# A quantised feed-forward stage written as turns, with five sequences under way and its wide rounding on another engine

## The chip, the core and the metric

The kernel runs on one core of a Trainium2 chip. The core has five engines, each with its own queue of instructions that it works through in order: TensorE (PE) multiplies matrices, VectorE (DVE), ScalarE (ACT) and GpSimd (POOL) work element by element, SyncE (SP) issues transfers between the main memory and SBUF, the on-chip memory. PE writes into PSUM, eight banks of 128 x 512 floats. Engines wait for one another by semaphores. The metric is the device time of one execution in microseconds (us).

## The reference, cut to what is touched

The model is a small decoder of two layers over 16 sequences of 128 positions and 1024 features. Its six parts run one after the other; each adds its result to its input and normalises. The third part, the feed-forward of the first layer, is the one that the change touches:

```python
def _dynamic_quant(x, inv_smooth):
    xs = x.astype(jnp.float32) * inv_smooth
    scale = jnp.maximum(jnp.max(jnp.abs(xs), axis=-1, keepdims=True) / QMAX, 1e-08)
    q = jnp.clip(jnp.round(xs / scale), -QMAX, QMAX)
    return (q, scale)
...
x_flat = x.reshape(-1, H).astype(jnp.bfloat16)
qg, sg = _dynamic_quant(x_flat, inv_gate)
qu, su = _dynamic_quant(x_flat, inv_up)
gate_out = _quant_gemm(qg, sg, w_gate, s_wgate)
up_out = _quant_gemm(qu, su, w_up, s_wup)
inter = jax.nn.silu(gate_out) * up_out
inter = jnp.clip(inter, -SWIGLU_LIMIT, SWIGLU_LIMIT).astype(jnp.bfloat16)
qi, si = _dynamic_quant(inter, inv_inter)
out = _quant_gemm(qi, si, w_down, s_wdown)
...
x = _layernorm(x + _L0_ffn_ref(x, ...), axis=-1)
```

H is 1024, the inner width 512, QMAX 127. So each position's row is turned into integers between -127 and 127 with a scale of its own, three times: for the gate product, for the up product, and for the down product.

## The kernel before

The stage `stage_quant` works on one sequence at a time: a tile of 128 positions (partitions) by 1024 features. It has no integer arithmetic; integers are floats that hold whole numbers, and each weight matrix is held as two parts (`w[n][0]`, `w[n][1]`) whose products are summed. For one sequence b it does this:

- `integers(b)`: SP loads x (line 60, four buffers); ACT casts it to bf16, xb (L669); for gate and for up POOL multiplies it by inv_gate or inv_up into xs (L673), and `quantise` follows on DVE: the maximum of the absolute values of a row, am (L603), the scale sc (L605), its reciprocal rc (L607), and the rounding (L608), which multiplies by rc and adds 12582912, so that the addition itself rounds.
- `first`: for gate and for up, `transposed` turns the 1024 columns in eight pieces of 128 (PE, L619) into two PSUM tiles t of four pieces each. ACT subtracts the constant again and writes the first half of qt (L621), DVE the second half (L623). Sixteen matmuls (L685: eight pieces of the contraction, two weight parts) give acc, 128x512. DVE scales gate's acc to g (L688), ACT applies silu (L689), DVE scales up's acc to u (L691), POOL multiplies g by u (L692), DVE clips to bf16, ib (L694), POOL multiplies by inv_inter to it (L696), and `quantise` runs over it.
- `second`: it is turned (four pieces, ACT writes qi, L621), sixteen matmuls over two halves of 512 columns give o (L705), DVE scales it to r (L708), POOL adds x (L709), and `layer_norm` finishes: DVE takes statistics in two halves (L85), their aggregate (L87) and the variance plus epsilon (L89), POOL takes the root ln_rs (L91), DVE normalises into x (L92). SP stores x (L711).

The loop takes a sequence's integers one step ahead, runs `first` of sequence b, then `second` of b-1. This is the order in which the program is written; a scheduler then orders each engine's instructions by its own estimate, except where the program ties them. `Ctx.ordered` (line 43) does that tying elsewhere in the kernel: it notes where it was called, and when the function that it returns is called, it ties every instruction of the given engines, written in between, to the one written before it on the same engine. `stage_quant` doesn't use it.

Pools hold the tiles in a number of buffers (`bufs`): a tile may be written once the tile that many places before it has been read to the end. Of PSUM, t has three banks, acc three, o two.

The stage before it (attention to a context, `stage_cross`) writes x1 to main memory, from where `stage_quant` loads; the stage after it (`stage_gqa`) loads x2, which `stage_quant` stores, and the memory of the weights of `stage_quant` is given free for its weights.

Of the kernel before, what the change touches and what calls it, by code (L numbers as in the profile page):

```python
# [23 lines left out]
P = 128  # L24
NB = 16
NT = NB * P
HID = 1024
# [4 lines left out]
class Ctx:  # L32
# [24 lines left out]
    def load(self, pool, src, b, tag="x", bufs=3):  # L57

        x = self.t(pool, [P, HID], tag, bufs=bufs)
        self.nc.sync.dma_start(x, src[b])  # L60
        return x
# [15 lines left out]
    return v.rearrange("(o n) -> o n", o=1).to_broadcast([parts, v.shape[0]])  # L77


def layer_norm(K, pool, src, dst):  # L80

    nc = K.nc
    st = K.t(pool, [P, 2, 6], "ln_st", bufs=2)
    for i in range(2):
        nc.vector.bn_stats(st[:, i, :], src[:, i * 512:(i + 1) * 512])  # L85
    mv = K.t(pool, [P, 2], "ln_mv", bufs=2)
    nc.vector.bn_aggr(mv, st.rearrange("p a b -> p (a b)"))  # L87
    ve = K.t(pool, [P, 1], "ln_ve", bufs=2)
    nc.vector.tensor_scalar(ve, mv[:, 1:2], LN_EPS, None, ALU.add)  # L89
    rs = K.t(pool, [P, 1], "ln_rs", bufs=2)  # L90
    nc.gpsimd.tensor_tensor(rs, ve, K.neghalf, ALU.pow)  # L91
    nc.vector.tensor_scalar(dst, src, mv[:, 0:1], rs, ALU.subtract, ALU.mult)  # L92

# [403 lines left out]
def stage_cross(K, rise, xmid, dst, piece):  # L497
# [6 lines left out]
    with ExitStack() as st:  # L504
# [3 lines left out]
        def risen(b):  # L508

            x, r = rise.got[b]  # L510
            if b + 2 < NB:
                rise.fetch(b + 2)
            for i in range(2):
                cols = slice(i * 512, (i + 1) * 512)
                pu = K.t(ps, [P, 512], "pu")
                nc.tensor.matmul(pu, xmid[:, b * P:(b + 1) * P], w["up"][:, cols], start=True, stop=True)
                nc.vector.tensor_tensor(r[:, cols], pu, r[:, cols], ALU.add)
            layer_norm(K, work, r, x)
            return x
# [54 lines left out]
        for b in range(NB):  # L574
            r = K.t(work, [P, HID], "ro")
            for i in range(2):
                if i == 0 and b + 1 < NB:
                    x1, kv1 = risen(b + 1), context(b + 1)
                nxt = None
                if i == 0:  # L580
                    nxt = attention(x, kv, 1)
                elif b + 1 < NB:
                    nxt = attention(x1, kv1, 0)
                attended(x, kv, i, ex, r)
                ex = nxt
            layer_norm(K, work, r, x)
            nc.scalar.dma_start(dst[b], x)
            piece(b)
            x, kv = (x1, kv1) if b + 1 < NB else (None, None)
# [3 lines left out]
MAGIC = 12582912.0  # L593
FFI = 512


def quantise(K, work, xs):

    nc = K.nc
    am = K.t(work, [P, 1], "am", bufs=4)
    nc.vector.tensor_reduce(am, xs, AX.X, ALU.max, apply_absolute_value=True)  # L603
    sc = K.t(work, [P, 1], "sc", bufs=6)
    nc.vector.tensor_scalar(sc, am, 1.0 / 127.0, 1e-8, ALU.mult, ALU.max)  # L605
    rc = K.t(work, [P, 1], "rc", bufs=4)
    nc.vector.reciprocal(rc, sc)  # L607
    nc.vector.tensor_scalar(xs, xs, rc, MAGIC, ALU.mult, ALU.add)  # L608
    return sc


def transposed(K, work, ps, q, n, tag, bufs=2):

    nc = K.nc
    qt = K.t(work, [P, n // P, P], tag, F32R, bufs=bufs)
    for h in range(n // 512):
        pt = K.t(ps, [P, 4, P], "t", bufs=3)
        for k in range(4):
            nc.tensor.transpose(pt[:, k, :], q[:, (4 * h + k) * P:(4 * h + k + 1) * P], K.ident)  # L619
        if h == 0:  # L620
            nc.scalar.activation(qt[:, 4 * h:4 * h + 4, :], pt, AF.Identity, bias=K.negmagic)  # L621
        else:
            nc.vector.tensor_scalar(qt[:, 4 * h:4 * h + 4, :], pt, MAGIC, None, ALU.subtract)  # L623
    return qt


def parts(K, hi, lo, v, eng):
# [30 lines left out]


def stage_quant(K, w, v, src, dst):  # L660
    nc, a = K.nc, K.a
    with ExitStack() as st:
        work = K.pool(st, "f_work", 2)
        ps = K.pool(st, "f_ps", 1, PSUM)
        def integers(b):

            x = K.load(work, src, b, bufs=4)
            xb = K.t(work, [P, HID], "xb", BF16)
            nc.scalar.copy(xb, x)  # L669
            qs = []  # L670
            for n in ("gate", "up"):
                xs = K.t(work, [P, HID], "xs", bufs=4)
                nc.gpsimd.tensor_tensor(xs, xb, v["inv_" + n], ALU.mult)  # L673
                qs.append((xs, quantise(K, work, xs)))
            return x, qs

        def first(x, qs):

            acc = []
            for (xs, _), n in zip(qs, ("gate", "up")):  # L680
                qt = transposed(K, work, ps, xs, HID, "qt")
                pa = K.t(ps, [P, FFI], "acc", bufs=3)
                for k in range(8):
                    for i in range(2):
                        nc.tensor.matmul(pa, qt[:, k, :], w[n][i][:, k, :], start=(k + i == 0), stop=(k + i == 8))  # L685
                acc.append(pa)
            g = K.t(work, [P, FFI], "g")
            nc.vector.scalar_tensor_tensor(g, acc[0], qs[0][1], v["s_wgate"], ALU.mult, ALU.mult)  # L688
            nc.scalar.activation(g, g, AF.Silu)  # L689
            u = K.t(work, [P, FFI], "u")  # L690
            nc.vector.scalar_tensor_tensor(u, acc[1], qs[1][1], v["s_wup"], ALU.mult, ALU.mult)  # L691
            nc.gpsimd.tensor_tensor(g, g, u, ALU.mult)  # L692
            ib = K.t(work, [P, FFI], "ib", BF16)
            nc.vector.tensor_scalar(ib, g, 10.0, -10.0, ALU.min, ALU.max)  # L694
            it = K.t(work, [P, FFI], "it")
            nc.gpsimd.tensor_tensor(it, ib, v["inv_inter"], ALU.mult)  # L696
            return x, it, quantise(K, work, it)

        def second(b, x, it, si):
            qt = transposed(K, work, ps, it, FFI, "qi", bufs=1)  # L700
            po = K.t(ps, [P, 2, 512], "o")
            for h in range(2):
                for k in range(4):
                    for i in range(2):
                        nc.tensor.matmul(po[:, h, :], qt[:, k, :], w["down"][i][:, k, h * 512:(h + 1) * 512],  # L705
                                         start=(k + i == 0), stop=(k + i == 4))
            r = K.t(work, [P, HID], "r", bufs=1)
            nc.vector.scalar_tensor_tensor(r, po.rearrange("p a b -> p (a b)"), si, v["s_wdown"], ALU.mult, ALU.mult)  # L708
            nc.gpsimd.tensor_tensor(r, r, x, ALU.add)  # L709
            layer_norm(K, work, r, x)  # L710
            nc.sync.dma_start(dst[b], x)  # L711


        ahead = integers(0)
        waiting = None
        for b in range(NB):
            now = ahead
            if b + 1 < NB:
                ahead = integers(b + 1)
            now = first(*now)  # L720
            if b:
                second(b - 1, *waiting)
            waiting = now
        second(NB - 1, *waiting)

# [538 lines left out]
class Front:  # L1264
# [62 lines left out]
    def product(self, l, bank):  # L1327
        t, j = self.place(l)
        if t < 0:
            return False  # L1330
        self.part(t, j, bank)
        if l == FIRST_ROUTED:
            self.first = routed(self.K, self.W, self.keep, lambda shape, tag: bank(shape, "gq"), self.xT[2], 1)
        return True
# [26 lines left out]
    def scaled(self, t, h):  # L1361

        nc, (raw, dst) = self.nc, self.scales[t]
        sl = slice(h * 512, (h + 1) * 512)
        hi = self.W["hi"]
        nc.vector.tensor_copy(hi, raw[:, sl])
        nc.vector.scalar_tensor_tensor(dst[:, sl], hi.bitcast(F32), self.lohi, raw[:, sl], ALU.mult, ALU.add)
# [499 lines left out]
```

## Time and profile before

| | us |
|---|---|
| median of three executions | 3445.27 (3441.66 to 3451.8) |
| the profiled execution, its own time | 3442.97 |
| its span | 3441.2 |
| busy in the span: PE, DVE, ACT, POOL | 3100.6, 1852.5, 1410.7, 898.8 |
| the stage: first cast of x to the end of the last normalisation | 596.36 to 905.77 |
| busy from 619.67 to 875.37: PE, DVE, ACT, POOL | 214.2, 173.4, 49.1, 131.2 |

The span is the time from the first to the last instruction in the profile. In the page's rows of slices the span is cut into 40 equal parts of 86 us; a digit is the busy share of an engine in tenths, and PEclk is the clock that PE was granted, in tenths of the full one. A row of windows gives a stretch, its length, and busy time and number of instructions of PE, its weight loads (PEld), DVE, ACT and POOL, then the granted clock, the busy share of the DMA engines and GB/s. A row of a group gives line, engine, operation, the tile written and the tiles read, shapes and count; then busy us and the mean of one in ns; then the engine's idle time just before these instructions and what ended it. A row of waits reads: who waited for whom, us in total, times, the longest. A row of the timeline: start and duration in us, engine, line, operation, tiles, count, and in brackets the idle time before it and what ended it.

Mean durations of single instructions in the stage (us): maximum of 128x1024 1.22, of 128x512 0.69; rounding of xs 0.85, of it 1.08 (0.48 at the least, 2.07 at the most); POOL's spreading of xs 2.15 to 2.24, its addition of x 2.40, g*u 1.29, it 1.17, root 0.55; ACT's cast 1.04, halves of qt 0.69, silu 0.63.

### The profile page before, as it was taken

The page shows a single profiled execution, that of the slowest core. Times are in us where ns is not written, and L with a number is a line of the kernel's source. Part 1 is how long each engine was busy: PE and PEld are TensorE (multiplying, and loading weights), DVE is VectorE, ACT ScalarE, POOL GpSimd, SP SyncE. Part 2 cuts the span into 40 slices and gives each one's busy share as a digit, 9 for nine tenths or more (in the row PEclk, how much of TensorE's full clock was granted, in tenths as well). Part 3 has the DMA queues.
Part 4 walks back from the last instruction along what each step waited for, and adds up shares of the span by engine and source line. Part 5 has one row for each costly group of instructions (what it writes and reads, how often), then busy time and mean ns, then how long its engine had stood idle before and what let it go on. Part 6 is the DMA issues. An engine that isn't in the chain of part 4 may idle for free.

```text
span 3441.2 us, 62967 instructions
## 1 busy us (share of the span) xinstructions
PE 3100.6 (90%) x24917; PEld 1679.0 (49%) x24917; DVE 1852.5 (54%) x5211; ACT 1410.7 (41%) x3610; POOL 898.8 (26%) x1087
## 2 busy tenths in 40 slices
PE   7887786888799999999998999999999999999998
PEld 3444453666455555555454444444444444444465
DVE  5875775666334454545233455555555555555555
ACT  3443432221132232334122555555555555555533
POOL 3334764455333233233011011111111111111122
PEclk8887998899899999998999999999999999999999
DMA  5001322111400010103221100000000000000044
GB/s 193 1 1 36 114 77 104 37 49 62 168 25 25 19 43 25 50 13 98 89 66 59 42 23 30 29 23 29 23 29 23 23 17 23 17 17 14 25 131 104
DMA packets 97216, 170.23 MB, mean 49 GB/s; under 512 B 14362, under 2 KB 55194, under 8 KB 96922
## 3 DMA queue, kind: packets, MB, share of 16 engines
q1 hardware_dynamic: 92858, 157.10, 14.4%
q10 hardware_dynamic: 4064, 9.11, 0.7%
q8 instruction: 197, 3.23, 0.4%
q14 instruction: 97, 0.79, 0.1%
HBM read 115.83 MB, written 51.64 MB: 49 GB/s over the span
## 4 chain that ended last, share of the span: by engine, by line
PE 57%; ACT 9%; DVE 6%; issue 2%; DMA 0%; POOL 0%; SPq 0%; DVEq 0%; POOLq 0%; ACTq 0%
PE p L794 8%; ACT th L1085 8%; PE s L1176 7%; PE pf L1070 7%; PE p L865 6%; PE p L1013 3%; PE m L1625 3%; PE gq L1212 3%; PE ff L1191 2%; PE t L843 2%; PE s L822 2%; PE p L807 2%; PE ff L1089 2%; PE s L1120 2%; PE c L854 1%
## 5 line engine op out<-in xcount | busy, mean ns | idle before, releaser
L1085 ACT ACTIVATE th<-pf 128x512 f32<-128x512 f32 x512 | 264.4, 602 | 276.9 <-PE pf L1070 276.8
L831 ACT ACTIVATE s<-s,nm 128x128 f32<-128x128 f32 x512 | 198.3, 389 | 251.7 <-DVE nm L828 221.7
L1205 POOL COPY hist<-gT 128x16 f32<-128x16 f32 x256 | 42.6, 198 | 934.9 <-DVE gT L1203 934.9
L1176 PE MATMUL s<-hb,aD 128*32 128x256 f32 x4096 | 276.1, 387 | 0.6 <-DVE aD L1164 0.6
L865 PE MATMUL p<-ga_Wo,cT 128*128 128x512 f32 x512 | 228.7, 595 | 0.0
L1158 ACT COPY pf<-enc 128x512 f32<-128x512 f32 x381 | 224.6, 590 | 8.1
L794 PE MATMUL p<-xT,ga_Wq 128*128 128x512 f32 x512 | 226.4, 597 | 0.0
L834 POOL TENSOR_TENSOR s<-s,rs 128x512 f32<-128x512 f32 x128 | 133.3, 1041 | 320.9 <-DVE rs L833 315.2
L1070 PE MATMUL pf<-R,waf 32*128 32x160 f32 x2032 | 181.4, 426 | 33.9 <-DVE R L1228 33.7
L794 PEld LDWEIGHTS p<-xT,ga_Wq 128*128 128x128 f32 x512 | 95.4, 190 | 113.8 <-issue 111.0
L865 PEld LDWEIGHTS p<-ga_Wo,cT 128*128 128x128 f32 x512 | 93.8, 190 | 113.8 <-issue 111.7
L1176 PEld LDWEIGHTS s<-hb,aD 128*32 128x32 f32 x4096 | 106.7, 109 | 84.3 <-DVE aD L1164 45.8
L1094 DVE TENSOR_REDUCE nm<-s 128x1 f32<-128x128 f32 x128 | 37.4, 292 | 203.3 <-PE s L1089 203.3
L1196 ACT ACTIVATE fs<-ff,rx 128x384 f32<-128x384 f32 x127 | 73.8, 581 | 173.2 <-DVE rx L1194 171.6
L1089 PE MATMUL s<-th,vaE 128*32 128x128 f32 x2048 | 109.0, 286 | 36.0 <-ACT th L1085 27.8
L845 DVE COPY pT<-t 128x512 f32<-128x512 f32 x128 | 87.9, 687 | 91.0 <-PE t L843 90.8
L1070 PEld LDWEIGHTS pf<-R,waf 32*128 32x128 f32 x2032 | 79.3, 182 | 99.4 <-DVE R L1228 74.2
L1089 PE MATMUL ff<-th,vaE 128*32 128x128 f32 x2048 | 109.6, 287 | 16.2
L91 POOL TENSOR_TENSOR ln_rs<-ln_ve,neghalf 128x1 f32<-128x1 f32 x64 | 37.9, 597 | 309.0 <-DVE ln_ve L89 292.3
L1013 PE MATMUL p<-xT,qT 128*128 128x512 f32 x256 | 115.8, 606 | 0.3 <-ACT qT L1008 0.2
L866 DVE TENSOR_TENSOR xr<-p,xr 128x512 f32<-128x512 f32 x32 | 22.1, 692 | 168.9 <-PE p L865 168.9
L685 PE MATMUL acc<-w_up,qt 128*128 128x512 f32 x256 | 79.6, 462 | 36.7 <-DVE qt L623 33.4
(392 smaller groups left out, 6794.8 us busy)
## 6 DMA issues: line engine op xcount, KB each, us to landing
x<-x SPq DMA_DIRECT2D x79, 512.0 KB, 3.6
xt<-xT SPq DMA_DIRECT2D x8, 1024.0 KB, 7.6
x<-x ACTq DMA_DIRECT2D x16, 512.0 KB, 2.6
xr<-x SPq DMA_DIRECT2D x16, 512.0 KB, 3.7
x<-xr SPq DMA_DIRECT2D x16, 512.0 KB, 2.6
x<-x SPq DMA_DIRECT2D x128, 64.0 KB, 2.4
xb<-r SPq DMA_DIRECT2D x16, 512.0 KB, 3.0
xb<-xb SPq DMA_DIRECT2D x16, 512.0 KB, 4.0
```

The costliest lines, as they stand in the source:

```text
L794: nc.tensor.matmul(pq, lhsT, xT[:, k].rearrange("p i t -> p (i t)"), start=(k == 0), stop=(k == 7))
L831: nc.scalar.activation(s[:, r, :], s[:, r, :], AF.Exp, bias=nm[:, r:r + 1], accum_out=sm[:, r:r + 1])
L834: nc.gpsimd.tensor_tensor(s, s, rs.unsqueeze(2).to_broadcast([P, 4, P]), ALU.mult)
L865: nc.tensor.matmul(po, cT[:, k, :], w["o"][h][:, k, :], start=(k == 0), stop=(k == 7))
L1013: nc.tensor.matmul(py, xT[:, k, b % 4, :], ys[:, k, :], start=(k == 0), stop=(k == 7))
L1070: nc.tensor.matmul(pf[:, k, first:first + n].rearrange("p b t -> p (b t)"), lhs[32 * k:32 * k + 32, :], rhs[32 * k:32 * k + 32, 32 * first ...
L1085: nc.scalar.activation(th.rearrange("p i (k t) -> p i k t", t=32), pf[:, :, 4 * g:4 * g + 4, :].rearrange("p k i t -> p i k t"), AF.Tanh)
L1089: nc.tensor.matmul(pe[32 * i:32 * i + 32, :], D["va"][:, 31 - b:63 - b], th[:, i, :], start=False, stop=(g % 2 == 1), skip_group_check=True)
L1158: nc.scalar.copy(pf[:, k], D["enc"][:, k])
L1176: nc.tensor.matmul(pg[32 * i:32 * i + 32, :], aD[:, 4 * g + i, :], D["hb"][:, 4 * g + i, :], start=(g == 0), stop=(g == 3), skip_group_che ...
L1212: nc.tensor.matmul(gq[32 * q:32 * q + 32, :], gT[:, c].rearrange("p e b -> p (e b)"), D["gs"][:, c, q * P:(q + 1) * P], start=False, stop= ...
L1625: nc.tensor.matmul(pm[:, h, :], xp[:, k, :], w[:, k, h * 512:(h + 1) * 512], start=(k + n == 0), stop=(k + n == 8))
```

## The change

The loop over sequences is replaced by turns. Turn b (from -2 to 17) handles parts of five sequences: the root, normalisation and store of b-2, the integers and the down product of b-1, both products of b, the integers of b+1, the cast and gate's spreading of b+2, and the load of b+3. PE, DVE, ACT and POOL are tied to the order in which the turn is written. Within a turn, the integers of the up product of b are turned before its gate product, those of the middle (it, of b-1) between the gate and the up product, and those of gate of b+1 before the down product of b-1. The rounding of xs goes from DVE to ACT (an Identity activation with rc as scale and the constant as bias, both columns of 128x1); the rounding of it stays on DVE. `quantise` and `transposed` become `scales` (without the rounding) and `turn` (which hands back the second half's subtraction, to be written later). `layer_norm` is split into `norm_sums` and `norm_root`, with unchanged instructions. x has five buffers instead of four, sc eight instead of six, and a column holding the constant is added.

```diff
+def norm_sums(K, pool, src):
...
+    return mv, ve
+def norm_root(K, pool, ve):
     rs = K.t(pool, [P, 1], "ln_rs", bufs=2)
+    K.nc.gpsimd.tensor_tensor(rs, ve, K.neghalf, ALU.pow)
+    return rs
...
-def quantise(K, work, xs):
+def scales(K, work, xs):
...
-    sc = K.t(work, [P, 1], "sc", bufs=6)
+    sc = K.t(work, [P, 1], "sc", bufs=8)
...
-    nc.vector.tensor_scalar(xs, xs, rc, MAGIC, ALU.mult, ALU.add)
-    return sc
+    return sc, rc
...
+        own = K.pool(st, "f_own", 1)
+        magic = K.t(own, [P, 1], "magic")
+        nc.vector.memset(magic, MAGIC)
+        X, XB, XS, SC, QT, ACC, G, U, IT, QI, O, R, MV, RS = ({} for _ in range(14))
+        def load(b):
+            X[b] = K.load(work, src, b, bufs=5)
+        def cast(b):
+            XB[b] = K.t(work, [P, HID], "xb", BF16)
+            nc.scalar.copy(XB[b], X[b])
+        def spread_out(b, n):
+            XS[b, n] = K.t(work, [P, HID], "xs", bufs=4)
+            nc.gpsimd.tensor_tensor(XS[b, n], XB[b], v["inv_" + n], ALU.mult)
+        def scaled(b, n):
+            SC[b, n], rc = scales(K, work, XS[b, n])
+            nc.scalar.activation(XS[b, n], XS[b, n], AF.Identity, bias=magic, scale=rc)
+        def turn(q, n, tag):
+            qt = K.t(work, [P, n // P, P], tag, F32R, bufs=2 if n > 512 else 1)
+            pts = []
+            for h in range(n // 512):
+                pt = K.t(ps, [P, 4, P], "t", bufs=3)
+                for k in range(4):
+                    nc.tensor.transpose(pt[:, k, :], q[:, (4 * h + k) * P:(4 * h + k + 1) * P], K.ident)
+                pts.append(pt)
+            nc.scalar.activation(qt[:, 0:4, :], pts[0], AF.Identity, bias=K.negmagic)
+            return qt, lambda: nc.vector.tensor_scalar(qt[:, 4:8, :], pts[1], MAGIC, None, ALU.subtract)
...
+        order = K.ordered((mybir.EngineType.PE, mybir.EngineType.DVE, mybir.EngineType.Activation, mybir.EngineType.Pool))
+        for b in range(3):
+            load(b)
+        for b in range(-2, NB + 2):
+            now, back, done, soon, far = (0 <= c < NB for c in (b, b - 1, b - 2, b + 1, b + 2))
+            if done:
+                R[b - 2] = K.t(work, [P, HID], "r", bufs=1)
+                nc.vector.scalar_tensor_tensor(R[b - 2], O[b - 2].rearrange("p a b -> p (a b)"), SC[b - 2, "it"], v["s_wdown"],
+                                               ALU.mult, ALU.mult)
+            if now:
+                QT[b, "up"], rest = turn(XS[b, "up"], HID, "qt")
+            if back:
+                SC[b - 1, "it"], rc = scales(K, work, IT[b - 1])
+                nc.vector.tensor_scalar(IT[b - 1], IT[b - 1], rc, MAGIC, ALU.mult, ALU.add)
+            if now:
+                rest()
+            if done:
+                nc.gpsimd.tensor_tensor(R[b - 2], R[b - 2], X[b - 2], ALU.add)
+            if soon:
+                scaled(b + 1, "gate")
+            if now:
+                product(b, "gate")
+            if soon:
+                spread_out(b + 1, "up")
+            if now:
+                G[b] = K.t(work, [P, FFI], "g")
+                nc.vector.scalar_tensor_tensor(G[b], ACC[b, "gate"], SC[b, "gate"], v["s_wgate"], ALU.mult, ALU.mult)
+            if back:
+                QI[b - 1], _ = turn(IT[b - 1], FFI, "qi")
+            if now:
+                nc.scalar.activation(G[b], G[b], AF.Silu)
+            if far:
+                cast(b + 2)
+            if soon:
+                scaled(b + 1, "up")
+            if now:
+                product(b, "up")
+            if done:
+                mv, ve = norm_sums(K, work, R[b - 2])
+                rs = norm_root(K, work, ve)
+            if far:
+                spread_out(b + 2, "gate")
+            if now:
+                U[b] = K.t(work, [P, FFI], "u")
+                nc.vector.scalar_tensor_tensor(U[b], ACC[b, "up"], SC[b, "up"], v["s_wup"], ALU.mult, ALU.mult)
+            if soon:
+                QT[b + 1, "gate"], rest = turn(XS[b + 1, "gate"], HID, "qt")
+            if now:
+                nc.gpsimd.tensor_tensor(G[b], G[b], U[b], ALU.mult)
+            if back:
+                product_down(b - 1)
+            if soon:
+                rest()
+            if done:
+                nc.vector.tensor_scalar(X[b - 2], R[b - 2], mv[:, 0:1], rs, ALU.subtract, ALU.mult)
+                nc.sync.dma_start(dst[b - 2], X[b - 2])
+            if 3 <= b + 3 < NB:
+                load(b + 3)
+            if now:
+                ib = K.t(work, [P, FFI], "ib", BF16)
+                nc.vector.tensor_scalar(ib, G[b], 10.0, -10.0, ALU.min, ALU.max)
+                IT[b] = K.t(work, [P, FFI], "it")
+                nc.gpsimd.tensor_tensor(IT[b], ib, v["inv_inter"], ALU.mult)
+        order()
```

`product` and `product_down` hold the matmuls of `first` and `second` as they were.

More of the change, by code (lines that the diff above doesn't have):

```diff
@@ L77, in spread @@
     return v.rearrange("(o n) -> o n", o=1).to_broadcast([parts, v.shape[0]])
-def layer_norm(K, pool, src, dst):
+def norm_sums(K, pool, src):
     nc = K.nc
@@ L89, in layer_norm @@
     nc.vector.tensor_scalar(ve, mv[:, 1:2], LN_EPS, None, ALU.add)
+    return mv, ve
+def norm_root(K, pool, ve):
     rs = K.t(pool, [P, 1], "ln_rs", bufs=2)
-    nc.gpsimd.tensor_tensor(rs, ve, K.neghalf, ALU.pow)
-    nc.vector.tensor_scalar(dst, src, mv[:, 0:1], rs, ALU.subtract, ALU.mult)
+    K.nc.gpsimd.tensor_tensor(rs, ve, K.neghalf, ALU.pow)
+    return rs
+def layer_norm(K, pool, src, dst):
+    mv, ve = norm_sums(K, pool, src)
+    K.nc.vector.tensor_scalar(dst, src, mv[:, 0:1], norm_root(K, pool, ve), ALU.subtract, ALU.mult)
 HY_L = 16
@@ L607, in quantise @@
     nc.vector.reciprocal(rc, sc)
-    nc.vector.tensor_scalar(xs, xs, rc, MAGIC, ALU.mult, ALU.add)
-    return sc
[L612 to L624, printed above, removed]
+    return sc, rc
 def parts(K, hi, lo, v, eng):
@@ L660, in stage_quant @@
 def stage_quant(K, w, v, src, dst):
-    nc, a = K.nc, K.a
+    nc = K.nc
     with ExitStack() as st:
@@ L664, in stage_quant @@
         ps = K.pool(st, "f_ps", 1, PSUM)
[L665 to L697, printed above, removed]
@@ L699, in second @@
-        def second(b, x, it, si):
-            qt = transposed(K, work, ps, it, FFI, "qi", bufs=1)
-            po = K.t(ps, [P, 2, 512], "o")
+        own = K.pool(st, "f_own", 1)
[7 more added lines that the diff above has]
+            nc.scalar.copy(XB[b], X[b])
@@ L702, in second, with product, product_down @@
+        def product(b, n):
+            ACC[b, n] = K.t(ps, [P, FFI], "acc", bufs=3)
+            for k in range(8):
+                for i in range(2):
+                    nc.tensor.matmul(ACC[b, n], QT[b, n][:, k, :], w[n][i][:, k, :], start=(k + i == 0), stop=(k + i == 8))
+        def product_down(b):
+            O[b] = K.t(ps, [P, 2, 512], "o")
             for h in range(2):
@@ L704, in second @@
                     for i in range(2):
-                        nc.tensor.matmul(po[:, h, :], qt[:, k, :], w["down"][i][:, k, h * 512:(h + 1) * 512],
+                        nc.tensor.matmul(O[b][:, h, :], QI[b][:, k, :], w["down"][i][:, k, h * 512:(h + 1) * 512],
                                          start=(k + i == 0), stop=(k + i == 4))
-            r = K.t(work, [P, HID], "r", bufs=1)
-            nc.vector.scalar_tensor_tensor(r, po.rearrange("p a b -> p (a b)"), si, v["s_wdown"], ALU.mult, ALU.mult)
@@ L709, in second @@
[L709 to L724, printed above, removed]
+        order = K.ordered((mybir.EngineType.PE, mybir.EngineType.DVE, mybir.EngineType.Activation, mybir.EngineType.Pool))
```

## The prediction, made before the changed kernel ran

> **What bounds the kernel now.** The page first, for where the stage lies: by the windows it runs from about 596 us (first input there) to 905.8 us, slices 7 to 10, and there neither PE nor its clock is full.
>
> ```profile
> PE   7887786888799999999998999999999999999998
> PEclk8887998899899999998999999999999999999999
> ```
>
> Next the windows. The repeating part goes from the gate product of sequence 1 (its first matmul starts at 619.68) to that of sequence 15 (875.38): 14 turns in 255.7 us, 18.26 us each.
>
> ```profile
> core 0: us, PE busy (x) PEld busy (x) DVE busy (x) ACT busy (x) POOL busy (x), PEclk, DMA share, GB/s
> ...
> 619.67:875.37 255.70, 214.22 (x949) 166.65 (x949) 173.38 (x318) 49.13 (x68) 131.17 (x82) 0.93 0.15 52
> ...
> 863.46:866.87 3.41, 1.17 (x6) 0.61 (x4) 2.64 (x7) 0.00 (x0) 2.02 (x2) 1.00 0.00 0
> 866.87:870.28 3.41, 3.23 (x8) 2.56 (x9) 2.96 (x7) 0.63 (x1) 0.00 (x1) 0.50 0.38 154
> ```
>
> Per turn: PE 15.3 busy of 18.3, DVE 12.4, POOL 9.4, ACT 3.5. PE is the fullest and still idles 3 us a turn, and the last two rows show what follows: in a 3.41 us window PE works 1.17 us, and in the next its clock is 0.50. So an idle stretch costs twice. The groups and waits of the stage (600 to 905 us) say who makes it idle:
>
> ```profile
> L685 PE MATMUL acc<-w_up,qt 128*128 128x512 f32 x256 | 79.6, 462 | 36.7 <-DVE qt L623 33.4 <-DVE ln_ve L89 1.9 <-ACT qt L621 0.4
> ...
> L608 DVE TENSOR_SCALAR xs<-xs,rc 128x1024 f32<-128x1024 f32 x32 | 26.0, 849 | 0.0
> ```
> ```profile
> PEld acc L685 <- DVE qt L623: 44.1, 21, 3.6
> ```
>
> The up product waits for the second half of its turned integers (qt, L623), which DVE has ready late. The timeline of one turn shows why:
>
> ```profile
> 858.11 2.42 POOL L709 TENSOR_TENSOR r<-r,x 128x1024 f32<-128x1024 f32 x1 [2.05 <-PE t L619]
> 858.74 2.07 DVE L608 TENSOR_SCALAR it<-it,rc 128x512 f32<-128x512 f32 x1
> ...
> 860.48 2.34 POOL L673 TENSOR_TENSOR xs<-xb,inv_gate 128x1024 f32<-128x1024 bf16 x1
> ...
> 862.78 2.15 POOL L673 TENSOR_TENSOR xs<-xb,inv_up 128x1024 f32<-128x1024 bf16 x1
> ...
> 864.96 1.22 DVE L603 TENSOR_REDUCE am<-xs 128x1 f32<-128x1024 f32 x1 [0.77 <-POOL xs L673]
> ...
> 866.30 0.69 DVE L623 TENSOR_SCALAR qt<-t 128x512 fp32r<-128x512 f32 x1
> ...
> 867.04 3.06 PEld L685 LDWEIGHTS acc<-w_up,qt 128*128 128x128 f32 x8 [2.84 <-DVE qt L623]
> ```
>
> DVE's queue puts two maxima (L603), both waiting for POOL, in front of qt. And a second thing: the rounding of it, 0.48 us in the undisturbed rows, took 2.07 because POOL's addition was running; it ended 0.28 us after that addition. The POOL instruction behind it took 2.34 instead of 2.15. So the two hold each other off for such DVE instructions (a scaling from SBUF to SBUF). Maxima, statistics and reads from PSUM keep their durations beside POOL.
>
> **The change, part by part.** *Rounding to ACT:* 32 DVE instructions go (26.0 us busy), 2 a turn. ACT gets the same 32; the output stage has exactly this form, Identity with bias and scale columns over 128x1024, at 1.242 us:
>
> ```profile
> L1639 ACT ACTIVATE xb<-os,ln_rs 128x1024 f32<-128x1024 f32 x16 | 19.9, 1242 | 43.4 <-POOL ln_rs L1636 43.2
> ```
>
> ACT then has 3.5+2.5=6.0 us of a turn, well under the rest. *Order:* no matmul, transposition, POOL or DMA instruction is added or dropped; a turn now handles up and gate of neighbouring sequences, and DVE, ACT, POOL and PE run in the written order. The fifth x buffer lets load b+3 be issued behind store b-2.
>
> *PE's floor:* 16 load-and-multiply pairs take 3.62 us at full clock (635.71), 3 products 10.9; 20 transpositions at 0.109 (5 in 0.70 at 861.16, less overlap) 2.2; some 0.3 for six changes between them: 13.4 a turn.
>
> *The DVE and POOL loop,* walked from the start of r (the L708 instruction of b-2) at 0, DVE steps from start to start as the timeline has them, since independent ones overlap by 0.07 to 0.09: r 1.19; maximum, scale, reciprocal of it 0.72+0.19+0.20, so the rounding wants to start at 2.3. But POOL's r+x begins 0.14 after r's end and takes 2.40, to 3.8, and holds the rounding until 3.8+0.28=4.1. Second half of up 0.61: 4.6. Gate's maximum, scale, reciprocal 1.5: 6.1. g 0.65: 6.8. Up's three 1.5: 8.3. Statistics, aggregate, epsilon 1.6: 9.9. u 0.67 and second half of gate 0.61: 11.2. Now the normalisation; POOL meanwhile: spreading of up until 5.9, the root from 10.05 to 10.6, spreading of gate b+2 to 12.7. In the cross stage such a normalisation waited for POOL's 1.49 and ended 0.55 behind it:
>
> ```profile
> 346.04 1.49 POOL L630 TENSOR_TENSOR w_up<-raw,w_up 128x512 fp32r<-128x512 f32 x1
> 346.48 1.60 DVE L92 TENSOR_SCALAR x<-r,ln_mv,ln_rs 128x1024 f32<-128x1024 f32 x1
> ```
>
> So it ends at 13.25, POOL's g*u (1.29) is held for up to that 0.55 and ends at 14.5, the clipping ib takes 0.43, and the next r starts at 14.9. That is the loop: **14.9 us**. Ends: 14.0 if neither hold falls so, 15.6 if nothing on DVE overlaps (some ten steps by 0.07).
>
> *Does PE keep up, and what is behind its waits?* it's transpositions are at 4.2 (after the rounding), up 4.7 to 8.35 (second half ready at 4.7), gate's transpositions to 9.3 (ACT's rounding ended at 7.4), down to 12.95 (qi at 8.1), up's next transpositions to 13.85 (their rounding, behind silu and the cast on ACT, ended at 11), gate product to 17.5; then it waits for the next rounding of it at 14.9+4.1=19.0. PE idles 1.5 us a turn. Behind that wait stands everything of PE, but DVE needs nothing of it before u at 9.9. Hidden: ACT's rounding, under products; if that cover went, 1.24 us each. The load: the normalisation ends at 13.25, store 2.6 us, load 3.6 (landings 3.5 to 3.7 in the stage), 19.6; ACT's cast wants it at 14.9+8.75=23.65. Spare 4.0 us.
>
> *Entry.* First cast 596.36 and first spreading to 599.62 stay. Maximum and reciprocal to 601.2, ACT's rounding to 602.5, gate's transpositions at half clock (1.94) to 604.4; up follows likewise (its rounding ends at 604.9, behind a cast) to 606.5; product 0 from 606.6 (now 608.55), up 0 from 610.7, transpositions of gate 1 and, after a 1.28 us table load in front of silu, those of up 1, to 616.6. The gate product of sequence 1 starts at 616.7 instead of 619.7: 3.0 gained (0 to 4). *End:* from the last gate product to the last normalisation 30.4 now (905.77-875.37). After: u 9.2, g*u, clipping and it 12.2, r of 14 to 13.5, rounding held by the addition to 16.4, transposition and qi 17.8, down at half clock as now (5.53) 23.3, r, addition, statistics, root, normalisation 30.2. Nothing: 0.2.
>
> *Sum* against the profiled execution (3442.97: span 3441.2 and 1.8 around it): 14 x (18.26-14.9) = 47.0, +3.0, +0.2 = 50.2. Span 3391.0, execution 3392.8. The median of the three runs, 3445.27, is 2.3 above the profiled one, so **3395**. The next stage's loads wait for this stage's end today and move with it.
>
> *The clock.* All eleven half-clock windows from 622 us on follow a window in which PE was busy at most half, and idle stretches of 1.60 and 1.86 us were followed by none. With 1.5 us idle a window is still 56% busy, so I take full clock. The Trainium skill ("TensorE: Matmul & The Clock Gate", the table of the two states) has the clock fall after an idle window of about 3.4 us; the rows fall earlier, at 1.17 us of work in 3.41, so the measurement decides. By that rule today's turns would never fall, and those after neither. The same page's section on a second failure mode says that frequent small idles can make the clock swing; no row here shows idles this short doing so.
>
> **Rivals.**
> - *PE becomes the bound.* If the holds at it and at the normalisation don't fall as walked, PE's 13.4 decides: 14 x 4.86 + 3.2 = 71.2, **3374**. For it: holds hit only 6 of 16 roundings of it now, and L92 was never held in this stage. Against: the written order puts r+x just ahead of the rounding every turn.
> - *The clock falls every turn.* One half-speed window costs 3.41/2=1.7; 13.4+1.5+1.7=16.6: 14 x 1.66 + 3.2 = 26.4, **3419**. For it: 1.5 is near the 2.13 that did it. Against: the rows above.
> - *The load lands late, slower than before.* ACT's cast stands ahead of up's rounding and gate's first half, on which PE waits; now a late x delays less, since four engines are not tied. From a landing of 3.6+4.0+3.4=11 us on, the turn is longer than 18.26. At the stage's entry one landing took 12.3 (the view of tile x; 3 MB of weights beside it): 19.6 a turn, 14 x 1.34 - 3.2 = 15.6 slower, **3461**. Against: 12 of 12 loads inside the stage in 3.5 to 3.7, DMA 15% busy.
> - *It doesn't do what it says:* the stage ends earlier but what follows starts no earlier, **3445**. Against: next stage's first loads are issued within 3 us of the last store.
>
> **Chances.** Loop 0.62 (own range 3382 to 3405, from 15.6 and 14.0 a turn), PE 0.15, clock 0.12, load 0.07, nothing 0.04. A measurement of this kernel tells some 0.3% (10 us) from no change. Faster 0.89, same 0.04, slower 0.07. The range takes in PE's floor and the clock: 3374 to 3420.
>
> **What would show it.** Gate products 14.9 us apart; maxima of xs no longer in front of qt; roundings on ACT at 1.24; the rounding of it at about 2 us nearly every turn and the normalisation over 1; PE's main wait at the transpositions of it; few clocks of 0.50. Wrong if PE never waits there (floor), if windows of 0.50 recur each turn, or if ACT's cast waits for DMA.

## The result, and the profile after

The changed kernel takes 3394.82 us (median of four executions, 3389.78 to 3401.36), the kernel before 3447.8 (four, 3441.66 to 3451.8): a ratio of 0.9846, 95% interval 0.9832 to 0.986. The profiled execution takes 3398.38 us with a span of 3396.6. In a second set of four, on another chip, the changed kernel takes 3393.34, at 0.9856 (0.9822 to 0.9889).

The page's two rows of slices say little here:

```profile
PE   7887887788899999999998999999999999999998
PEclk8887899999899999898999999999999999999999
```

The turns lie in slices 8 to 10 (a slice is 84.9 us), and PE's digits there, 7, 8 and 8, are near those of before. The windows, cut from the gate product of sequence 1 to that of sequence 15, tell it apart:

```profile
620.33:826.22 205.89, 186.99 (x956) 153.69 (x954) 180.11 (x290) 78.03 (x97) 138.17 (x83) 1.00 0.17 60
```

The same 14 turns take 205.9 us instead of 255.7, 14.71 each instead of 18.27. PE is busy for 13.36 us of a turn, the clock is 1.00 throughout (0.93 before), and DVE, at 12.9 a turn, is nearly as full as PE. Next the groups of the stage (590 to 862 us) and its waits:

```profile
L698 PE MATMUL acc<-w_up,qt 128*128 128x512 f32 x256 | 62.4, 396 | 0.0
...
L680 ACT ACTIVATE xs<-xs,magic,rc 128x1024 f32<-128x1024 f32 x32 | 39.8, 1244 | 100.9 <-DVE rc L615 100.9
...
L762 DVE TENSOR_SCALAR x<-r,ln_mv,ln_rs 128x1024 f32<-128x1024 f32 x16 | 29.6, 1850 | 1.3 <-POOL ln_rs L95 1.3
L756 POOL TENSOR_TENSOR g<-g,u 128x512 f32<-128x512 f32 x16 | 26.4, 1652 | 2.1 <-DVE u L752 2.1
...
L721 DVE TENSOR_SCALAR it<-it,rc 128x512 f32<-128x512 f32 x16 | 25.2, 1578 | 0.6
```
```profile
PE t L689 <- DVE it L721: 23.1, 14, 4.2
...
ACT xb L671 <- DMA x<-x: 20.8, 1, 20.8
```

The up product waits for nothing any more (0.0, where it idled 36.7). PE's wait has moved to the transpositions of it. Three instructions have grown longer: the rounding of it from 1.08 to 1.58 us, the normalisation from 0.81 to 1.85, g*u from 1.29 to 1.65. One turn in the timeline, then the last one:

```profile
704.33 2.17 POOL L675 TENSOR_TENSOR xs<-xb,inv_gate 128x1024 f32<-128x1024 bf16 x1
704.91 2.14 DVE L762 TENSOR_SCALAR x<-r,ln_mv,ln_rs 128x1024 f32<-128x1024 f32 x1
706.44 1.75 POOL L756 TENSOR_TENSOR g<-g,u 128x512 f32<-128x512 f32 x1
708.22 0.43 DVE L768 TENSOR_SCALAR ib<-g 128x512 bf16<-128x512 f32 x1 [1.18 <-POOL g L756]
708.57 1.28 DVE L715 SCALAR_TENSOR_TENSOR r<-o,sc,s_wdown 128x1024 f32<-128x1024 f32 x1
709.98 2.37 POOL L725 TENSOR_TENSOR r<-r,x 128x1024 f32<-128x1024 f32 x1
711.05 1.58 DVE L721 TENSOR_SCALAR it<-it,rc 128x512 f32<-128x512 f32 x1
712.78 0.63 PE L689 MATMUL t<-ident,it 128*128 128x128 f32 x4 [1.54 <-DVE it L721]
...
723.43 1.28 DVE L715 SCALAR_TENSOR_TENSOR r<-o,sc,s_wdown 128x1024 f32<-128x1024 f32 x1
...
842.07 0.63 PE L689 MATMUL t<-ident,it 128*128 128x128 f32 x4 [4.22 <-DVE it L721]
...
843.53 6.71 PE L705 MATMUL o<-w_down,qi 128*128 128x512 f32 x16 [0.84 <-ACT qi L691]
```

POOL's r+x ends at 712.35 and the rounding of it, begun at 711.05, 0.28 later. The spreading of gate ends at 706.50, the normalisation 0.55 later. Then POOL's g*u takes 1.75, and DVE waits 1.18 us for it before the clipping. From r to r (708.57 to 723.43) it is 14.86.

**Where the time went.** The stage, from its first cast (600.77) to the end of the last normalisation (857.26), takes 256.49 us; before it took 309.42. That is 52.9 less: 49.8 in the 14 turns, 3.8 at the entry (19.56 from the first cast to the gate product of sequence 1, where it was 23.32), and 0.7 lost at the end (31.04 instead of 30.38). The profiled span is only 44.6 shorter, as the stage began 4.4 later in this execution and what follows it took 3.9 longer; those parts have the same instructions in both kernels, and over all profiled runs here the stage's first cast lies anywhere from 596 to 610. So a part of some us is read from the stage, not from the span. The medians differ by 53.0.

### The profile page after: what moved, and what is told of

It reads as the page before. It is cut to its first block, busy times and chain, and to the rows that moved or that the text cites. A ratio compares the mean times of both kernels' runs of the same rounds, so it can differ in the third digit from the quotient of the medians.

```text
span 3396.6 us, 62991 instructions
## 1 busy us (share of the span) xinstructions
PE 3080.5 (91%) x24917; PEld 1671.7 (49%) x24917; DVE 1858.2 (55%) x5180; ACT 1443.7 (43%) x3642; POOL 904.3 (27%) x1087
## 3 DMA queue, kind: packets, MB, share of 16 engines
q1 hardware_dynamic: 92858, 157.10, 14.5%
## 4 chain that ended last, share of the span: by engine, by line
PE 61%; ACT 10%; DVE 9%; POOL 6%; issue 4%; DMA 1%; SPq 0%; POOLq 0%; DVEq 0%; ACTq 0%
PE p L841 8%; ACT th L1132 8%; PE s L1223 8%; PE pf L1117 7%; PE p L912 6%; PE p L1060 3%; PE m L1672 3%; PE gq L1259 3%; PE ff L1238 2%; PE t L890 2%; PE s L869 2%; POOL xs L675 2%; PE p L854 2%; PE ff L1136 2%; PE s L1167 2%
## 5 line engine op out<-in xcount | busy, mean ns | idle before, releaser
L869 PE MATMUL s<-kT,qT 32*128 32x128 f32 x1024 | 107.7, 312 | 0.0
```

The lines of the kernel that those rows point to most:

```text
L869: nc.tensor.matmul(psc[n][:, r, :], qT[sl, 4 * kc + r, i, :], kT[sl, kc, i, :], start=True, stop=True)
```

## The experiments

Each run's ratio is to the kernel before on the same chip in the same set (its median was 3451.25, 3446.02 and 3445.78 in the three sets). "Turn" is the mean pitch of the gate products of sequences 1 to 15, "steady" the pitch once the first turns are over, "stage" the time from the first cast to the end of the last normalisation.

**Each half of the change alone.** First the changed kernel with xs rounded on DVE again:

```diff
-            nc.scalar.activation(XS[b, n], XS[b, n], AF.Identity, bias=magic, scale=rc)
+            nc.vector.tensor_scalar(XS[b, n], XS[b, n], rc, MAGIC, ALU.mult, ALU.add)
```

> The changed kernel with the rounding of xs back on VectorE, at the same place in the written order. Theory (the turn is a loop through VectorE and GpSimd): two more VectorE steps of 0.7 us each turn, both at moments when GpSimd is idle, so no further hold: turn 14.86 -> 16.3 us, 14 x 1.4 = 20 us more than the changed kernel, about 3415. Rival (the written order alone brings the gain, the move of the rounding lies beside the path): turn stays within 0.3 of 14.9, time about 3395.

3418.62 us, 0.9906 (0.9883 to 0.9929); turn 16.16, stage 274.98. Two DVE steps of 0.75 lengthen the turn by 1.45: DVE's row is what counts, as expected.

Then the kernel before with nothing but the rounding of xs on ACT (`magic` is a column with the constant; the rounding of it, without that argument, stays on DVE):

```diff
-    nc.vector.tensor_scalar(xs, xs, rc, MAGIC, ALU.mult, ALU.add)
+    if magic is not None:
+        nc.scalar.activation(xs, xs, AF.Identity, bias=magic, scale=rc)
+    else:
+        nc.vector.tensor_scalar(xs, xs, rc, MAGIC, ALU.mult, ALU.add)
...
-                qs.append((xs, quantise(K, work, xs)))
+                qs.append((xs, quantise(K, work, xs, magic)))
```

> The kernel before with only the rounding of xs moved to ScalarE, order left to the scheduler. Theory: the late step in the old turn is VectorE's second half of qt, queued behind two maxima that wait for GpSimd; the roundings stood behind it, so their going shortens the turn by at most the 1.4 us that they take: turn 16.9 to 18.0, time 3425 to 3445. Rival (the rounding on ScalarE is what brings the gain): turn at or under 15.5, time 3405 or less.

3445.5 us, 0.9991 (0.9977 to 1.0005); turn 17.62, stage 303.19. The turn came as expected, the time half a us above what was expected. The rival, that the rounding does it alone, falls. The 6 us that the trace shows can't be told from nothing in the times.

**The order, its tie and its content.** The changed kernel without the call that ties it:

```diff
-        order()
```

> The changed kernel, with the instructions written in the same turns, but not tied to that order. Theory: the order of the queues is what shortens the turn, and the scheduler's own order puts waiting maxima ahead again: turn 15.5 to 17.5, time 3404 to 3432. Rival (splitting into turns and the ScalarE rounding suffice, the tie is idle): turn 14.9 within 0.3, time 3395 within 5.

3438.66 us, 0.9961 (0.9945 to 0.9978); turn 17.18, stage 294.53, the turns between 14.2 and 20.5. It is somewhat slower than I expected (3404 to 3432). The scheduler orders the instructions anew, and PE, ACT and POOL wait for other things; its waits (640 to 840 us) show among others one that the tied kernel has at the entry alone:

```profile
ACT xb L671 <- DMA x<-x: 56.1, 10, 8.4
```

The waiting maxima of xs, which the theory named, aren't among these waits: DVE waits for POOL's r+x (28.7 us) and for it (16.1 us). So the run shows that the order is needed, but not the mechanism that I had expected.

The converse, the kernel before with its own written order tied:

```diff
+        order = K.ordered((mybir.EngineType.PE, mybir.EngineType.DVE, mybir.EngineType.Activation, mybir.EngineType.Pool))
...
+        order()
```

> The kernel before with its four engines tied to the order in which it is written (integers of b+1, both products of b, then the down product and normalisation of b-1). Theory: what shortens the turn is the interleaved arrangement and not the tie as such; the old written order puts the product's whole chain (u, g*u, clipping, it, its rounding) in series ahead of the next r: turn 22 to 26, time 50 to 110 us more than before. Rival (any fixed order beats the scheduler's): turn at or under 16.

3607.83 us, 1.0464 (1.0441 to 1.0486): slower, and by more than I allowed for; turn 28.78. Its timeline shows where PE waits:

```profile
715.08 1.29 DVE L85 BATCH_NORM_STATS2 ln_st<-r 128x6 f32<-128x512 f32 x2 [2.56 <-POOL r L709]
...
717.46 2.61 DVE L92 TENSOR_SCALAR x<-r,ln_mv,ln_rs 128x1024 f32<-128x1024 f32 x1 [0.66 <-POOL ln_rs L91]
...
724.83 0.68 DVE L623 TENSOR_SCALAR qt<-t 128x512 fp32r<-128x512 f32 x1
725.57 3.78 PE L685 MATMUL acc<-w_gate,qt 128*128 128x512 f32 x8 [11.26 <-DVE qt L623]
```

A whole normalisation, both maxima and both roundings of xs stand in front of the second half of qt, and PE waits 11.26 us for it (135.3 us in 12 such waits from 650 to 1000 us). That is another step than the product's chain that the expectation named. A tie is worth what the written order is worth.

**The two holds.** If r+x holds the rounding of it, and gate's spreading the normalisation, moving POOL's steps should take the holds from the loop. Up's spreading goes ahead of r+x, and gate's to the end of the turn:

```diff
+            if soon:
+                spread_out(b + 1, "up")
             if done:
                 nc.gpsimd.tensor_tensor(R[b - 2], R[b - 2], X[b - 2], ALU.add)
...
-            if soon:
-                spread_out(b + 1, "up")
...
-            if far:
-                spread_out(b + 2, "gate")
...
                 nc.gpsimd.tensor_tensor(IT[b], ib, v["inv_inter"], ALU.mult)
+            if far:
+                spread_out(b + 2, "gate")
```

> The changed kernel with two GpSimd instructions moved in the written order, nothing else: spreading of up ahead of the addition r+x, spreading of gate b+2 behind the last instruction of the turn. Theory: the rounding of it is then held by the spreading (until about 3.6 instead of 4.1 us into the turn), g*u starts as soon as u is there (10.7 instead of 12.7), the next r starts at 12.5 to 13; the loop falls under TensorE's own 13.4, which decides: turn 13.4 to 13.9, about 3377 to 3382. Rival (TensorE's work or its waits for something else set 14.86): turn unchanged, 3395. Third: the holds fall elsewhere and cost as much: 14.5 to 15.

3380.23 us, 0.9794 (0.9769 to 0.9819), faster than both kernels; turn 13.35, stage 238.42. Its windows over the 14 turns:

```profile
630.10:817.00 186.90, 185.31 (x956) 154.40 (x954) 169.64 (x290) 78.12 (x97) 134.96 (x84) 1.00 0.18 66
```

PE is busy for 185.31 of 186.90 us: nearly its floor. Ten of the 14 pitches are 13.18 to 13.23, four 13.7 to 13.8. DVE's work fell by 10 us with no instruction gone, since the roundings of it now take 1.42 and the normalisations 1.35; PE's waits for it are almost gone (groups from 600 to 870 us, waits from 640 to 820):

```profile
L721 DVE TENSOR_SCALAR it<-it,rc 128x512 f32<-128x512 f32 x16 | 22.8, 1423 | 0.6
...
L760 DVE TENSOR_SCALAR x<-r,ln_mv,ln_rs 128x1024 f32<-128x1024 f32 x16 | 21.6, 1351 | 1.3 <-POOL ln_rs L95 1.3
```
```profile
PE t L689 <- DVE it L721: 1.3, 3, 0.4
```

The moves do two things at once. They shorten the holds, and they take g*u out from behind gate's spreading in POOL's queue. How much of the gain is due to each isn't shown.

Either move alone:

> The changed kernel with only the spreading of up moved ahead of the addition r+x on GpSimd. Theory (the loop through VectorE and GpSimd, with holds): the rounding of it is held until 3.6 instead of 4.06 us into the turn, the rest of the loop stays: turn 14.86 -> 14.3 to 14.5, time about 3387 to 3390. Rival (only the late spreading of gate mattered in the run with both moves): 14.86, 3395.

> The changed kernel with only the spreading of gate b+2 moved to the end of the turn on GpSimd. Theory: g*u no longer waits for it and the next r starts earlier, but the spreading now delays the addition r+x and with it the held rounding of it by about 1.5: turn 13.9 to 14.6, time about 3382 to 3391. Rival (each move alone reaches TensorE's floor): 13.4, 3376 to 3380.

The first: turn 14.36 (steady 14.50), stage 251.94, 3396.49 us, 0.9847 (0.9827 to 0.9867). The second: turn 14.15 (steady 14.38), stage 249.49, 3396.8 us, 0.9849 (0.9831 to 0.9867). The turns came as expected, the times did not (3387 to 3390 and 3382 to 3391 were expected): the gains of 4.5 and 7.0 us in the stage don't show in the medians, whose sets of four spread by 6 to 9 us. In the second a new wait takes a part back, as its timeline shows: with gate's spreading ahead of r+x, up's spreading is late for its maximum.

```profile
733.90 1.22 DVE L611 TENSOR_REDUCE am<-xs 128x1 f32<-128x1024 f32 x1 [1.66 <-POOL xs L675]
```

**it rounded on ACT.** This removes the first held instruction instead of the holder, and 1.58 us of DVE's turn:

```diff
-                nc.vector.tensor_scalar(IT[b - 1], IT[b - 1], rc, MAGIC, ALU.mult, ALU.add)
+                nc.scalar.activation(IT[b - 1], IT[b - 1], AF.Identity, bias=magic, scale=rc)
```

> The changed kernel with the rounding of it on ACT as well: DVE loses 1.58 us of work in a turn of 14.86, and the instruction that POOL's r+x holds is gone. ACT should need 0.65 us for 128x512 (half of its 1.244 for 128x1024), so it is ready some 0.9 us earlier, and PE, which waited 1.5 us for it, waits 0.6 or less. Theory (the row of DVE and POOL sets the turn): 13.4 to 14.0 us a turn, 3375 to 3390 us. Rival (PE's wait is set by POOL's r+x and what follows it, which stay): 14.5 us or more, 3390 us or more.

3384.02 us, 0.982 (0.9794 to 0.9845); turn 13.90 (steady 14.1), stage 244.76. Time and turn came as expected. The turn gains half of what DVE loses, and PE still waits 0.6 to 0.8 us for it. DVE now waits for POOL in its timeline:

```profile
709.37 0.43 DVE L768 TENSOR_SCALAR ib<-g 128x512 bf16<-128x512 f32 x1 [1.17 <-POOL g L756]
...
715.67 1.22 DVE L611 TENSOR_REDUCE am<-xs 128x1 f32<-128x1024 f32 x1 [0.67 <-POOL xs L675]
```

The second wait is new: up's spreading, behind r+x, now comes late for a DVE that is earlier. The other, and the hold of the normalisation (2.14 as before), stay. On ACT the rounding of it took 0.82 us, not the 0.65 that I had from half of 1.244.

With both moves as well:

> The kernel with both of POOL's steps moved, and the rounding of it on ACT as well. Theory: with both moves PE already sets the turn (185.31 us busy of 186.90), so taking 1.58 us from DVE gives nothing: 13.2 to 13.5 us a turn, and a time within 4 us of the kernel with both moves (3380 us). Rival (DVE's row still counts): 12.9 us a turn or less, 3373 us or less.

3371.37 us, 0.9794 (0.977 to 0.9818); turn 13.19, stage 233.87. Its windows:

```profile
621.01:805.73 184.72, 184.72 (x955) 154.66 (x954) 149.50 (x276) 91.06 (x111) 133.19 (x84) 1.00 0.20 69
```

By the records PE is never idle, so nothing on DVE can shorten this turn further. That relief of DVE gives nothing was too strong, though: the turn is 0.16 us shorter than with both moves alone, as the four pitches of 13.7 to 13.8 are gone, and the stage is 4.6 us shorter. The time misses the theory's 4 us around 3380 and falls in the rival's figure (3373 or less), which I had set in us and not as a ratio; by the ratios this kernel and the one with both moves are not told apart.

**Does a lost clock cost?** The prediction said that an idle stretch costs twice. With the rounding on DVE, in turns tied and regular, PE idles 3.0 us in seven of the 14 pitches, and 27.3 us of half clock fall within the turns. Matmuls that nothing needs, put into that wait, keep PE busy (the edit cut to them; the down product takes its tile o here instead of in `product_down`):

```diff
-            nc.scalar.activation(XS[b, n], XS[b, n], AF.Identity, bias=magic, scale=rc)
+            nc.vector.tensor_scalar(XS[b, n], XS[b, n], rc, MAGIC, ALU.mult, ALU.add)
...
-            O[b] = K.t(ps, [P, 2, 512], "o")
...
+            if back:
+                O[b - 1] = K.t(ps, [P, 2, 512], "o")
+            if now and back:
+                for j in range(8):
+                    nc.tensor.matmul(O[b - 1][:, j % 2, :], QT[b, "gate"][:, j % 4, :], w["gate"][0][:, j % 4, :], start=True, stop=True)
             if back:
                 QI[b - 1], _ = turn(IT[b - 1], FFI, "qi")
```

> The changed kernel with xs rounded on DVE again, and in PE's wait ahead of it's transpositions eight matmuls whose result is overwritten (tile o, taken earlier in the turn): some 2 us of PE work that nothing needs. With DVE's rounding alone the trace showed turns of 16.2 us and 27.3 us of half clock within the turns. Theory: DVE's and POOL's row sets the turn, and the half clock of PE lies in time that PE has to spare: the half clock goes (5 us or less is left of it) and the turn stays at 16.0 to 16.5 us, the time at 3413 to 3424 us. Rival (an idle stretch of PE is paid again by the slower clock after it): half of 27.3 us comes back, 0.98 us a turn over 14 turns, so turns of 15.1 to 15.4 us and some 3405 us.

3416.28 us, 0.9926 (0.9899 to 0.9952); turn 16.08 (steady 16.4), stage 277.28. The 14 turns in windows, first with idle stretches, then filled:

```profile
625.78:852.02 226.24, 198.74 (x955) 162.62 (x954) 200.84 (x318) 49.02 (x70) 138.90 (x83) 0.94 0.15 54
```
```profile
622.60:847.66 225.06, 215.34 (x1068) 174.10 (x1066) 199.99 (x316) 48.80 (x70) 138.78 (x82) 1.00 0.16 54
```

The clock goes from 0.94 to 1.00, DVE's 200 us stay, and the length stays. The rival (27.3/2 = 13.6 us back) falls: the slower matmuls lay in time that PE had to spare. In both kernels r follows r at 16.4 us in the steady turns, while in the unfilled one the gate products' pitch swings between 13.5 and 19.2. The filled stage is not shorter as a whole (277.28 against 274.98), since its entry and end took 3.5 us longer.

The same was tried earlier on the kernel before, with eight such matmuls between the halves of its up product (the edit cut to them; `po` is the down product's tile, taken ahead of `first`):

```diff
+                    if n == "up" and k == 3 and po is not None:
+                        for j in range(8):
+                            nc.tensor.matmul(po[:, j % 2, :], qt[:, j % 4, :], w[n][0][:, j % 4, :], start=True, stop=True)
```

> The kernel before with eight idle matmuls (1.8 us at full clock) written between the halves of each up product, into the PSUM tile of the down product, which the down product overwrites later: TensorE is kept busy in its wait, so that its clock does not fall. Theory (the old turn too is set by VectorE and GpSimd, TensorE's slow windows lie in idle time): half-clock time in the 14 turns falls from 37.5 us to 15 or less, and the turn changes by at most 0.4 us: time within 6 us of before or a little above. Rival (an idle stretch costs twice, in idle time and in clock): 37.5 / 2 = 18.8 us less, turn 17.0, time 16 to 20 us less than before.

3488.62 us, 1.0119 (1.0097 to 1.0141); turn 20.6, half clock 47.8 us instead of 37.5. The half clock grew instead of going, so the condition of the test wasn't met: the untied scheduler placed much else anew, and this settles nothing about what the clock costs.

**The changed kernel once more**, beside the last three:

> The changed kernel once more, as a yardstick on the chip of these runs: turns of 14.7 to 14.9 us, a time of 0.983 to 0.987 of the kernel before.

3393.34 us, 0.9856 (0.9822 to 0.9889); turn 14.68, entry 20.03, end 30.10, stage 255.64.

## Why the prediction came true, step by step

**The time.** 3395 was forecast, 3394.82 came. The stage gained 52.9 where the sum said 50.2. That the time still agrees to 0.2 us is chance: a fourth execution put the median of the kernel before 2.5 us above that of the three from which the sum started, which makes up for nearly all of this.

**The loop, 14.9: right.** Steady turns take 14.8 to 14.9. From the start of r, walked and measured: r+x ends at 3.8 and 3.78, the rounding of it at 4.1 and 4.06, gate's maximum starts at 4.6 and 4.58, g at 6.1 and 6.09, up's maximum at 6.8 and 6.74, statistics at 8.3 and 8.32, gate's spreading ends at 12.7 and 12.78, the normalisation at 13.25 and 13.33, g*u at 14.5 and 14.48, the next r starts at 14.9 and 14.86. What the sum left out is that the loop needs three turns to fill: the first r stands in the turn of sequence 2, and the first two pitches after the gate product of sequence 1 took 14.21 and 13.38. So the 14 gave 49.8 instead of 47.0.

**The holds: right.** They fall at the two instructions and at the times that were walked. With POOL's steps moved the turn falls nearly to PE's floor, though no instruction is gone, so POOL's order sets the turn; what the holds alone are worth in it stays open, as said above. The Trainium skill ("SBUF — State Buffer", "Who interferes with whom") has GpSimd share one pair of ports with those DVE instructions that use two, whoever issues first keeping it for its whole instruction, and ACT wait for nobody. The trace agrees: the held DVE instructions end 0.28 and 0.55 us behind POOL's, and the rounding on ACT takes 1.236 to 1.25, as foreseen from 1.242, whatever POOL does.

**The rounding on ACT: right**, in the prediction's setting. DVE's two steps are worth 1.45 us in the tied turn and 0.65 in the old order (18.27 to 17.62). The written, tied order with DVE's rounding is worth 2.1 (18.27 to 16.16). Together they give 3.56, more than 0.65 and 2.1: with the old order PE waits for the second half of qt as before (30.6 us from 640 to 840 us, where it was 30.0), whatever was taken off DVE elsewhere.

**PE's idle 1.5 us, and its place: right** (1.43 to 1.55, at the transpositions of it). The floor of 13.4 was 13.19 with nothing in the way.

**Entry and end: mis-sized, in opposite directions.** The entry gained 3.8 (3.3 in the second profile) instead of 3.0; by the first the gate product of sequence 0 came 0.34 earlier than walked and sequence 1's another 0.43. At the end the term of 0.2 gained was 0.7 lost (0.3 gained in the second profile): PE waits 4.22 us for the last rounding of it, and the down product after it, taken as 5.53 from the profile of before, took 6.71: the half clock lasted until 849.52, 6.0 us into it (in the profile of before for 3.4 us of it). In the second profile it took 5.30, with 3.0 us of half clock. Its length hangs on when the clock comes back. That the two terms together gave 3.1 where the sum had 3.2 is luck.

**"An idle stretch costs twice": not borne out as a rule.** The clock does fall, and in the filled kernel it stays up, but there DVE and POOL set the turn and the lost clock cost nothing. At the end of the stage, where DVE waits 5.26 us for PE, it does cost: the last down product takes 6.71 us, one in the turns 3.9. Whether it cost something in the kernel before is open; the one run that was to tell it rearranged the stage. The sum didn't use it, as it took turn for turn. The prediction named the short stretches that no half clock followed (1.60 and 1.86 us), but not the long ones: of 2.78, 3.15 and 3.02 us, from 697.88, 715.11 and 790.24.

**The rivals.** *PE the bound* failed on its condition, since the holds fell as walked; where they were moved its price held: 13.2 to 13.35 a turn, and 3371 and 3380 us around the forecast 3374. *The clock falls each turn*: no half clock within the turns. *The late load*: ACT's cast waited for DMA once, at the entry. *It doesn't do what it says*: the time followed the stage.

**Not run alone: the fifth buffer of x.** In the kernel before, ACT's cast waited six times for a load (600 to 905 us); within the changed turns it never does.

```profile
ACT xb L669 <- DMA x<-x: 16.6, 6, 4.6
```

Five buffers alone don't bring this, as the untied turns with five wait 56.1 us. But no run has the tied turns with four, so what the fifth is worth isn't shown.

## What to carry to other kernels

When a stage is a cycle over four engines, walk one turn instruction by instruction from the trace, with the holds between engines written in as waits: here it gave the turn to 0.1 us and named the two instructions whose move brings the rest (0.9846 to 0.9794). An instruction moved to an idle engine is worth its length only if the order lets the next one follow; a tie is worth what its order is worth, and the old one tied was 4.6% slower. Look for the next bound before the next edit: with PE busy for nearly the whole turn, taking the rounding of it off DVE brought 0.16 us a turn.

## What was not expected of the hardware

- DVE and POOL instructions hold one another in both directions: a normalisation that is 0.81 us alone took 2.14 behind POOL's spreading, and POOL's g*u, which came behind that, 1.75 instead of 1.29.
- Half clock can be free: 27.3 us of it within 14 turns, taken away, changed the turn of 16.4 us not at all. It was not free at the end of the stage, where PE was waited for.
- On ACT half the width costs well over half: 0.82 us for 128x512 against 1.244 for 128x1024.
- Idle stretches of 1.43 to 1.55 us in PE, one in each of twelve turns, lowered the clock in none of them. The Trainium skill ("TensorE: Matmul & The Clock Gate", "HAM oscillation — how this bites in real kernels") puts the bound at gaps of some 3.4 us; with xs rounded on DVE six of seven gaps of 3.0 were followed by half clock, so the measurement decides. In each profile the changes of the clock lie whole multiples of 3.41 us apart, and in this stage the fall goes with how long PE was busy in the stretch before it. The first row is the stretch ahead of one fall; the seventh gap lay across the other two, and the clock stayed:

```profile
756.26:759.67 3.41, 0.51 (x5) 0.54 (x6) 3.21 (x7) 0.00 (x0) 3.34 (x3) 1.00 0.48 154
...
786.98:790.39 3.41, 1.89 (x9) 1.23 (x7) 2.82 (x6) 0.00 (x0) 2.80 (x3) 1.00 0.53 185
790.39:793.80 3.41, 1.91 (x11) 1.69 (x12) 3.34 (x5) 0.69 (x1) 3.38 (x2) 1.00 0.34 125
```

From 590 to 860 us of the 14 profiles, half clock followed all 65 stretches at full clock in which PE was busy for 0.42 or less, and none in which it was busy for 0.44 or more. Elsewhere in the kernel it also followed fuller ones, so this is seen for this stage alone.
